# First image of a convolution and attention kernel: combined taps made earlier, 42 convolution products ahead of the maxima, and the queries' transfers asked for apart from those of the relative logits

## The chip, the cores and the metric

The kernel runs on one core of one Trainium2 chip, in float32. The metric is the device time of one execution in microseconds. Each version is run three times and its median is given. Beside that there is one execution taken by the hardware profiler, whose trace is what the profile shows.

## What is computed

The input is `x`, 8 images of 32 x 32 positions with 256 channels. Layer 0 works on each image by itself:

- a group normalization of the channels (groups of 8) over the whole image;
- a 3 x 3 convolution from 256 to 192 channels;
- beside it, attention over the 1024 positions with 8 heads of 8 channels. Its logits are `q.k` plus two relative terms, one that depends on the horizontal distance and the query, and one that depends on the vertical distance and the query;
- the two results are put side by side (192 + 64 channels) and added to `x`.

Layer 1 is a single-head attention over the 1024 positions of each image, and then a mixture of 8 experts of which 2 are taken for each image, with layer norms between. In the reference's words, the part that the change touches is

```python
logits = jnp.einsum('bnid,bnjd->bnij', qf, kf) + rel_w + rel_h
weights = jax.nn.softmax(logits, axis=-1)
conv_out = lax.conv_general_dilated(x, conv_w, (1, 1), 'SAME', ...) + conv_b
```

## The kernel before

**Stages.** The kernel takes the images one after the other. Of an image, the stages are: normalization (`norm_steps`), queries, keys, values and relative logits (`input_steps`), the attention of layer 0 with the convolution woven in (`conv_layer_attention`), and the attention of layer 1 (`attention_layer`). While one image is in its attention, the normalization and the input steps of the next one are run in pieces between the steps of the current one (`ahead`, `more`, `fill`). After the eighth image comes the expert stage.

**The convolution** is done along rows in groups of four outputs with the transform of a fast convolution: `conv_weights` makes six combined sets of taps (`convw`) from the three taps of a row, once in the program, and `by_fours` makes six combined inputs (`gdif`) for each image. `conv_weights` is six instructions of VectorE of 1152 elements (L277 to L290) with ScalarE's scalings between them. The convolution of an image is then 72 products (L515, `conv_steps`). A product is one matmul instruction in the program and two matmuls in the trace, since it is float32; the same holds for every matmul here. Every 12 products fill one PSUM tile `pc`, which ScalarE copies out (L524), and GpSimd adds the result to the image `T`.

**The attention of layer 0** is cut into four units (two groups of four heads, two halves of the queries). Each unit has a tile `F` of 128 partitions, which holds the moving operand of its logits in blocks of 32 rows for each head: 16 rows of the vertical relative logits (`F<-rh`), 8 rows of the queries (`F<-kq`), 8 rows of the horizontal relative logits, which later also take the maxima (`F<-rwd`, `F<-mb`). These rows are put there by DMA from the tiles `rh` and `kq` and from the DRAM tile `rwd`. In all that is 8 + 8 + 8 transfers for a unit, issued by SyncE (SP). The stationary operand is `km`: keys, copied in by 16 transfers `km<-kq` (L431), beside patterns of zeros and ones that GpSimd makes once, at the start, in 32 small instructions (`key_patterns`, L260 and L261).

**The steps of a unit.** A unit has 8 steps of *scoring*: two times two products `lg<-km,F` (L583), each pair followed by a maximum on VectorE (L591, 128x1024 elements). Then its maxima are turned and put into `F` (`fold`, L607 to L613), and 8 steps of *weighing* follow: products `st<-F,km` (L623), exponentials on ScalarE (L631) and products with the values (L640). Weighing lags by 10 steps (`lead = NT + LAG`), so in the first 10 steps of an image nothing is weighed, and what is left of the convolution is spread over them. Before the first step, `first` products of the convolution are issued:

```python
            first = min(left, 3 * KC)
            conv.run(first)
```

For the first image all 72 products are left, so 6 stand in front, and then 7, 7, 7, 7, 7, 7, 6, 6, 6, 6 follow the scores of the ten steps. For every other image 36 of 72 are left at that point, the rest having run in the attention of layer 1 of the image before: 6 in front and 3 after the scores of each step.

**The prologue.** The first image has no image before it in whose attention its normalization and input steps could run. Its order on TensorE and VectorE is the order of the calls: normalization, the first 12 pieces of `input_steps` (`pk` L396, `kq` L406 on ScalarE and L413 on VectorE, `pvv` L417, `vall` L436), then the tables of the relative logits (`reld_steps`, L236, eight instructions on VectorE), then one piece of `input_steps` after the other with three pieces of `other` behind each. `other` is `by_fours` and after it `conv_weights`. The pieces of `input_steps` in this part are the relative logits: products `prel` (L468) in four lots, each copied out of PSUM by VectorE and ScalarE together (L480, L482: two lots to `rw`, two to `rh`), then the transposes `tpw` (L493) and their copies to `rwq` (L495 VectorE, L497 ScalarE).

**What orders the rest.** TensorE keeps the order of the calls all through the eight images, VectorE in the prologue alone. Every other queue is ordered by the framework's scheduler, SP's and GpSimd's too. A queue runs in order: an instruction that waits holds those behind it. An SP transfer also waits until the transfer eight places before it has landed, since eight semaphores are used in turn.

**The buffers of F.** The tag `F` has three buffers, and the taps, the normalized image `x`, the relative logits `rw`, the units' `F` and two tiles of layer 1 take them in turn. In the first image the taps, `x` and `rw` have the three, and the first unit's `F` gets that of `x`: its transfers wait for the last instruction of `by_fours`.

Of the kernel before, what the change touches and what calls it, by code (L numbers as in the profile page):

```python
# [20 lines left out]
NT = S // P  # L21
KC = C // P
NH, DH, DK = 8, 8, 64
HG = 4
# [12 lines left out]
def kernel(  # L37
# [26 lines left out]
    nc = tc.nc  # L64
# [27 lines left out]
    with ExitStack() as ph:  # L92
# [32 lines left out]
        for n, table in (("h", key_rel_h), ("w", key_rel_w)):  # L125
# [19 lines left out]
        taps = work.tile([P, 4096], FP, tag="F", name="taps", bufs=3)[:, 0 : 9 * KC * CO]  # L145
        nc.scalar.dma_start(
            out=taps.rearrange("p (n o) -> p n o", o=CO), in_=conv_w.rearrange("a b (k p) o -> p (a b k) o", p=P)
# [121 lines left out]
        def conv_weights(taps):  # L269


            taps = taps.rearrange("p (a b n) -> p b a n", a=3, b=3)
            w0, w1, w2 = (taps[:, i] for i in range(3))
            cw = [convw[:, v] for v in range(NV)]
            nc.scalar.mul(cw[4], w0, 0.25)
            nc.scalar.copy(cw[5], w2)
            nc.vector.tensor_tensor(cw[1], w0, w2, ALU.add)  # L277
            yield
            nc.vector.tensor_tensor(cw[0], cw[1], w1, ALU.add)
            nc.scalar.mul(cw[0], cw[0], -1.0 / 6)  # L280
            yield
            nc.vector.tensor_tensor(cw[1], cw[1], w1, ALU.subtract)
            nc.scalar.mul(cw[1], cw[1], -1.0 / 6)
            yield
            nc.vector.scalar_tensor_tensor(cw[3], w2, 4.0, w0, ALU.mult, ALU.add)
            yield
            nc.vector.scalar_tensor_tensor(cw[2], w1, 2.0, cw[3], ALU.mult, ALU.add)
            nc.scalar.mul(cw[2], cw[2], 1.0 / 24)
            yield
            nc.vector.scalar_tensor_tensor(cw[3], w1, -2.0, cw[3], ALU.mult, ALU.add)  # L290
            nc.scalar.mul(cw[3], cw[3], 1.0 / 24)
            yield
# [92 lines left out]
        def input_steps(b, held):  # L385
# [3 lines left out]
            xn = held["xn"].rearrange("p k a c j x -> p k (a c j x)")  # L389
            kq = work.tile([P, S], FP, tag="kq", name="kq")  # L390
# [35 lines left out]
            for g in range(NG):  # L426
                for a in range(2):
                    for hl in range(HG):
                        r = 32 * ((hl + 2 * a) % HG) + 16
                        h = g * HG + hl  # L430
                        nc.sync.dma_start(  # L431
                            out=KM[g][r : r + DH, a].rearrange("p e k -> p (e k)"),
# [18 lines left out]
            rw = [rw[:, g * S : (g + 1) * S] for g in range(NG)]  # L451
            rwd = [drw.tile([P, S], FP, tag="rwd", name="rwd", bufs=2 * NG) for _ in range(NG)]
            rwq = work.tile([P, NT, NG, P], FP, tag="rwq", name="rwq")
            held.update(kq=kq, rh=rh, rwd=rwd, rwq=rwq)
            for which in range(2):
                for half in range(2):
                    prs = lg_tile("prel")
# [30 lines left out]
            for t2 in range(NT // 2):  # L488
# [7 lines left out]
                else:  # L496
                    nc.scalar.copy(rwq[:, t2 * 2 : t2 * 2 + 2], tp)  # L497
                yield 0.43, 0
            held["units"] = [Unit(0, kq, rh, rwd)]

        def conv_steps(b, place):

# [38 lines left out]
        class Unit:  # L541


            def __init__(self, n, kq, rh, rwd):
                self.g, self.half = divmod(n, 2)
                g, cols = self.g, slice(self.half * 512, self.half * 512 + 512)
                self.rh = rh[g][:, cols]


                self.F = f_tile("F")  # L550
                for a in range(2):
                    for hl in range(HG):
                        r = 32 * ((hl + 2 * a) % HG)
                        h = g * HG + hl
                        nc.sync.dma_start(
                            out=self.F[r : r + 16, a],
                            in_=rh[g][a * 64 + hl : a * 64 + 64 : HG, cols].unsqueeze(1).to_broadcast([16, 4, 512]),
                        )
                        nc.sync.dma_start(
                            out=self.F[r + 16 : r + 24, a],  # L560
                            in_=kq[DK + h * DH : DK + (h + 1) * DH, cols].unsqueeze(1).to_broadcast([DH, 4, 512]),
                        )
                for a in range(2):
                    for hl in range(HG):
                        r = 32 * ((hl + 2 * a) % HG)
                        nc.sync.dma_start(
                            out=self.F[r + 24 : r + 32, a],
                            in_=rwd[g].rearrange("(e j h) s -> h j e s", e=4, h=HG)[hl, :, :, cols],
                        )
                self.mx = work.tile([P, 4, HG], FP, tag="mx", name="mx", bufs=2)  # L570
                self.pts = {}
                self.po = None
# [108 lines left out]
        def conv_layer_attention(b, units, kq, rh, rwd, rwq, conv, early, ahead, more):  # L681

            at = work.tile([P, NT, DK], FP, tag="at", name="at")
            units.append(Unit(1, kq, rh, rwd))
            left = conv.left
            lead = NT + LAG  # L690
            first = min(left, 3 * KC)
            conv.run(first)
            left -= first
            for s in range(NU * NT + lead + 2):
                u, j = divmod(s, NT)
                w, k = divmod(s - lead, NT)
                g, l = divmod(s - lead - 1, NT)
                score, weigh, gather = u < NU, 0 <= w < NU, 0 <= g < NU


                if score:
                    units[u].score(2 * j, rwq)
                    if weigh:
                        units[w].weigh(k, (1,), st_tile)
                        units[w].weigh(k, (3,), st_tile)
                    if gather and l:
                        units[g].gather(l, (0, 1))
                    units[u].score(2 * j + 1, rwq)
                    if weigh:
                        units[w].weigh(k, (0,), st_tile)  # L710
                        units[w].weigh(k, (2,), st_tile)
                    if gather:
                        units[g].gather(l, (2, 3) if l else (0, 1, 2, 3))
                else:
                    if weigh:
                        units[w].weigh(k, (0,), st_tile)
                        units[w].weigh(k, (2,), st_tile)
                        units[w].weigh(k, (1, 3), lg_tile)
                    if gather:
                        units[g].gather(l, (0, 1, 2, 3))  # L720
                if g == NU:
                    more(KC, 0)
                if 0 <= g and g <= NU and l == 0 and g > 0:
                    units[g - 1].settle(at)
                if g == NU:
                    more(NT // 2, 0)
                if not weigh:
                    todo = -(-left // (lead - s))
                    conv.run(todo)
                    left -= todo  # L730
                if s == 5:
                    early()
                if s > NU * NT:
                    next(ahead, None)
                if s % NT == 0 and 0 < u <= NU:
                    units[u - 1].fold(u - 1)
                if s % NT == 0 and 0 < u < NU - 1:
                    units.append(Unit(u + 1, kq, rh, rwd))

            aT = pt_tile("aT")[0:DK, 0:S]  # L740
            for q in range(2):
                tp = st_tile("tpa").rearrange("p (j t) -> p j t", j=4)
                for j in range(4):
                    nc.tensor.transpose(tp[0:DK, j, :], at[:, q * 4 + j, :], ident)
                dst, src = aT[:, q * 512 : (q + 1) * 512], tp[0:DK].rearrange("p j t -> p (j t)")
                if q == 0:
                    nc.vector.tensor_copy(dst, src)
                else:
                    nc.scalar.copy(dst, src)
            more(KC, 0)  # L750
            pp = st_tile("pp").rearrange("p (t c) -> p t c", c=DK)
            for t in range(NT):
                nc.tensor.matmul(pp[:, t, :], lhsT=aT[:, t * P : (t + 1) * P], rhs=aw, start=True, stop=True)
            nc.vector.tensor_tensor(T[b][:, :, CO:C], pp, T[b][:, :, CO:C], ALU.add)
            more(0, 4)
# [199 lines left out]
        with tc.manual_schedule(engines={mybir.EngineType.PE, mybir.EngineType.DVE}):  # L955
            held = {}
            half_w, half_h, reld_steps = tables()
            for _ in norm_steps(0, held):
                pass
            KM = key_patterns()  # L960
            steps = input_steps(0, held)
            for _ in range(4 + NT):
                next(steps)
            reld_steps()
            other = chain(by_fours(held["xn"]), conv_weights(taps))
            for _ in steps:
                for _ in range(3):
                    next(other, None)
            for _ in other:
                pass  # L970
        with tc.manual_schedule(engines={mybir.EngineType.PE}):
            conv = Conv(0)
            means = []
            for b in range(B):
# [12 lines left out]
                now, held = held, {}  # L987
# [319 lines left out]
```

## Time and profile before

| what | value |
|---|---|
| median of 3 runs | 2448.43 us |
| the runs | 2446.56, 2448.43, 2452.04 us |
| the profiled execution | 2444.67 us, with a span of 2442.9 us |
| mean clock granted to TensorE | 0.981 |
| TensorE matmul (PE) | 2314.1 us busy, 95% of the span |
| VectorE (DVE) | 1485.5 us, 61% |
| ScalarE (ACT) | 1026.1 us, 42% |
| GpSimd (POOL) | 475.6 us, 19% |

The profile page gives busy time for each engine (matmuls are pipelined, so a busy PE isn't PE at its peak), a row of 40 slices of the span for each engine with the clock that TensorE was granted, and the costliest groups of instructions. The trace behind it answers with timelines (start, duration, engine, line, operation, and in brackets how long the engine had been idle and what released it), with tables of busy time by stretch, and with the shortest, median and longest duration of the instructions of one line.

### The profile page before, as it was taken

The numbers are of one execution on the slowest core, as the hardware profiler recorded it, in microseconds if no ns is written. First come the engines' busy times: TensorE is split into PE (matmuls) and PEld (weight loads), VectorE is DVE, ScalarE is ACT, GpSimd is POOL, SyncE is SP. The second block draws the span as 40 slices with busy tenths as digits, with TensorE's granted clock in tenths as the row PEclk, the third lists the DMA queues.
The fourth block names the chain that finished last, engine by engine and source line by source line (L and its number), as shares of the span: only waits on it lengthen the run. The fifth ranks groups of instructions, "written<-read, shape, count | busy, mean of one in ns | idle before, by whom it ended". The sixth has DMA issues, their size and how long they took to land. (4 is left out here: it accounts for less than half of the span.)

```text
span 2442.9 us, 41840 instructions
## 1 busy us (share of the span) xinstructions
PE 2314.1 (95%) x17273; PEld 1299.7 (53%) x17273; DVE 1485.5 (61%) x2661; ACT 1026.1 (42%) x1717; POOL 475.6 (19%) x446
## 2 busy tenths in 40 slices
PE   5999999999999999999999999999998879999998
PEld 4535643564366436643663376337632546666665
DVE  7776487548755875587467746774774434444443
ACT  2255336433643464346335732563266323222232
POOL 3202130213031202210230023002301032222221
PEclk7999999999999999999999999999999989999999
DMA  4521242134222412240324032403240032121210
GB/s 124 82 40 27 41 97 39 35 46 90 32 43 57 80 22 51 57 85 9 58 70 72 4 57 70 72 4 57 60 66 2 23 121 69 69 69 69 70 60 26
DMA packets 71468, 135.82 MB, mean 56 GB/s; under 512 B 12000, under 2 KB 24168, under 8 KB 69232
## 3 DMA queue, kind: packets, MB, share of 16 engines
q1 hardware_dynamic: 65488, 115.47, 23.7%
q0 software_dynamic: 3056, 15.73, 1.9%
q8 instruction: 136, 2.23, 0.4%
q10 hardware_dynamic: 2736, 1.97, 0.3%
q14 instruction: 52, 0.43, 0.1%
HBM read 53.43 MB, written 25.17 MB: 32 GB/s over the span
## 5 line engine op out<-in xcount | busy, mean ns | idle before, releaser
L591 DVE TENSOR_REDUCE my<-lg 128x32 f32<-128x1024 f32 x512 | 618.5, 1223 | 161.8 <-PE st L623 125.9
L631 ACT ACTIVATE PT<-st 128x512 f32<-128x512 f32 (+1 forms) x944 | 541.6, 633 | 306.2 <-PE st L623 301.7
L623 PE MATMUL st<-F,km 32*128 32x512 f32 x2048 | 545.2, 641 | 17.2 <-DMA F<-mb 11.9
L583 PE MATMUL lg<-km,F 24*128 24x512 f32 x2048 | 534.9, 637 | 6.1 <-DMA F<-kq 3.7
L640 PE MATMUL po<-PT,vall 128*32 128x256 f32 (+1 forms) x3200 | 315.1, 453 | 2.9 <-ACT PT L631 2.4
L583 PEld LDWEIGHTS lg<-km,F 24*128 24x128 f32 x2048 | 156.0, 183 | 186.5 <-issue 112.1
L515 PE MATMUL pc<-convw,gdif 128*128 128x192 f32 x1152 | 236.1, 345 | 11.5 <-ACT m L524 8.7
L640 PEld LDWEIGHTS po<-PT,vall 128*32 128x32 f32 x3200 | 66.9, 108 | 314.6 <-issue 280.1
L515 PEld LDWEIGHTS pc<-convw,gdif 128*128 128x128 f32 x1152 | 186.8, 192 | 81.5 <-issue 59.9
L623 PEld LDWEIGHTS st<-F,km 32*128 32x128 f32 x2048 | 177.5, 184 | 96.3 <-issue 43.5
L1220 PE MATMUL phd<-n2T,w 128*128 128x512 f32 x512 | 223.7, 594 | 0.0
L1237 PE MATMUL py<-w,hT 128*128 128x256 f32 x1024 | 223.6, 379 | 0.0
L1237 PEld LDWEIGHTS py<-w,hT 128*128 128x128 f32 x1024 | 194.6, 190 | 33.3 <-issue 7.4
L311 POOL TENSOR_TENSOR T<-T,l0b 128x2048 f32<-128x2048 f32 x8 | 36.4, 4546 | 633.5 <-PE tpx L304 633.5
L1220 PEld LDWEIGHTS phd<-n2T,w 128*128 128x128 f32 x512 | 97.0, 191 | 114.9 <-issue 107.7
L1244 DVE TENSOR_TENSOR r<-py,n 128x256 f32<-128x256 f32 x64 | 27.1, 423 | 215.0 <-PE py L1237 215.0
L863 PE MATMUL po<-pt,qkv 128*128 128x256 f32 x512 | 116.6, 381 | 11.3 <-DVE pt L855 11.3
L524 ACT COPY m<-pc 128x384 f32<-128x384 f32 x48 | 23.0, 479 | 247.3 <-PE pc L515 247.3
L1227 ACT ACTIVATE hT<-phd,b1c 128x512 f32<-128x512 f32 x128 | 86.3, 686 | 96.5 <-PE phd L1220 96.3
L841 DVE TENSOR_REDUCE nm<-lg 128x1 f32<-128x1024 f32 x64 | 78.1, 1220 | 77.5 <-PE lg L832 77.5
L780 POOL TENSOR_TENSOR T<-T,n 128x256 f32<-128x256 f32 x64 | 47.1, 743 | 372.8 <-DVE n L775 372.8
L832 PE MATMUL lg<-qkv 128*128 128x512 f32 x256 | 119.1, 593 | 0.0
(250 smaller groups left out, 2627.6 us busy)
## 6 DMA issues: line engine op xcount, KB each, us to landing
F<-rh SPq DMA_DIRECT2D x256, 128.0 KB
F<-kq SPq DMA_DIRECT2D x256, 64.0 KB
F<-rwd SPq DMA_DIRECT2D x256, 64.0 KB
w<-in_L_ffn_W_dram SPq DMA_DIRECT2D x32, 512.0 KB
rwd<-rw SPq DMA_DIRECT2D x16, 512.0 KB
Td<-T POOLq DMA_DIRECT2D x8, 1024.0 KB, 8.3
T<-Td SPq DMA_DIRECT2D x8, 1024.0 KB
out_dram<-yo SPq DMA_DIRECT2D x16, 512.0 KB
```

The costliest lines, as they stand in the source:

```text
L515: nc.tensor.matmul(pc[:, v, :], lhsT=gflat[:, 2 * pair + v, kc, at : at + P], rhs=convw[:, 2 * pair + v, dy, kc * CO : (kc + 1) * CO], sta ...
L583: nc.tensor.matmul(lg[:, a, :], lhsT=self.F[r : r + 24, a, 0, i * P : (i + 1) * P], rhs=KM[self.g][r : r + 24, a].rearrange("p e k -> p (e ...
L591: nc.vector.tensor_reduce(my[:, :, hl], lg.rearrange("p a (y x) -> p y a x", y=WW), AX.XY, ALU.max)
L623: nc.tensor.matmul(st[:, i, :] if len(heads) > 1 else st, lhsT=KM[self.g][r : r + 32, a, e, :], rhs=self.F[r : r + 32, a, e, :], start=Tru ...
L631: nc.scalar.activation(self.pts[j][:, hs, :], st, AF.Exp)
L640: nc.tensor.matmul(self.po[32 * hl : 32 * hl + 32, cols], lhsT=vall[:, j, h * (DH + 1) : h * (DH + 1) + 32], rhs=self.pts[j][:, hl, cols], ...
L832: nc.tensor.matmul(lg[:, h, :], lhsT=qk[0][:, i * P : (i + 1) * P], rhs=qk[1][:, h * 512 : (h + 1) * 512], start=True, stop=True,)
L841: nc.vector.tensor_reduce(nm, lg, AX.X, ALU.max, negate=True)
L863: nc.tensor.matmul(po[:, 0:IB], lhsT=v1[:, jc, :], rhs=pt[:, jc, :], start=jc == 0, stop=jc == NT - 1)
L1220: nc.tensor.matmul(phd, lhsT=ws[k][0][:, kc, f * P : (f + 1) * P], rhs=n2T[:, kc, q * 512 : (q + 1) * 512], start=kc == 0, stop=kc == KC - 1,)
L1227: nc.scalar.activation(hT[:, k * NF + f, :], phd, AF.Gelu, bias=b1c[:, f, k * B + b : k * B + b + 1])
L1237: nc.tensor.matmul(py, lhsT=hT[:, k * NF + f, j * P : (j + 1) * P], rhs=ws[k][1][:, f, :], start=k == 0 and f == 0, stop=k == TOPK - 1 and ...
```

## The change

There are three edits.

1. **Transfers of a unit in two parts.** `Unit` asks for the 8 transfers `F<-kq` when it is made. A new method `relate` asks for the 8 `F<-rh` and the 8 `F<-rwd`. For the first unit of an image the unit is now made as soon as `kq` is there, ahead of the relative logits, and `relate` is called at the end of `input_steps`. For the other units the two calls follow each other. Before, `F<-rh` and `F<-kq` alternated.
2. **`first = max(0, left - 3 * lead)`** in place of `min(left, 3 * KC)`. For the first image that is 72 - 30 = 42 products in front, and 3 after the scores of each of the ten steps. For the other images it is 36 - 30 = 6, as it was.
3. **The prologue's order.** `other` is now `conv_weights` and after it `by_fours`, and it is begun with the first piece of `input_steps`.

```diff
-            held.update(kq=kq, rh=rh, rwd=rwd, rwq=rwq)
+            held.update(kq=kq, rh=rh, rwd=rwd, rwq=rwq, units=[Unit(0, kq)])
...
-            held["units"] = [Unit(0, kq, rh, rwd)]
+            held["units"][0].relate(rh, rwd)
...
-            def __init__(self, n, kq, rh, rwd):
+            def __init__(self, n, kq):
                 self.g, self.half = divmod(n, 2)
-                g, cols = self.g, slice(self.half * 512, self.half * 512 + 512)
+                self.cols = slice(self.half * 512, self.half * 512 + 512)
+                self.F = f_tile("F")
+                for a, hl, r in self.places():
+                    h = self.g * HG + hl
+                    nc.sync.dma_start(
+                        out=self.F[r + 16 : r + 24, a],
+                        in_=kq[DK + h * DH : DK + (h + 1) * DH, self.cols].unsqueeze(1).to_broadcast([DH, 4, 512]),
+                    )
+            def places(self):
+                return [(a, hl, 32 * ((hl + 2 * a) % HG)) for a in range(2) for hl in range(HG)]
+            def relate(self, rh, rwd):
+                g, cols = self.g, self.cols
                 self.rh = rh[g][:, cols]
...
+                for a, hl, r in self.places():
+                    nc.sync.dma_start(
+                        out=self.F[r : r + 16, a],
+                        in_=rh[g][a * 64 + hl : a * 64 + 64 : HG, cols].unsqueeze(1).to_broadcast([16, 4, 512]),
+                    )
+                for a, hl, r in self.places():
+                    nc.sync.dma_start(
+                        out=self.F[r + 24 : r + 32, a],
+                        in_=rwd[g].rearrange("(e j h) s -> h j e s", e=4, h=HG)[hl, :, :, cols],
+                    )
...
-            units.append(Unit(1, kq, rh, rwd))
+            units.append(Unit(1, kq))
+            units[1].relate(rh, rwd)
...
-            first = min(left, 3 * KC)
+            first = max(0, left - 3 * lead)
...
-                    units.append(Unit(u + 1, kq, rh, rwd))
+                    units.append(Unit(u + 1, kq))
+                    units[u + 1].relate(rh, rwd)
...
-            for _ in range(4 + NT):
-                next(steps)
-            reld_steps()
-            other = chain(by_fours(held["xn"]), conv_weights(taps))
-            for _ in steps:
-                for _ in range(3):
+            other = chain(conv_weights(taps), by_fours(held["xn"]))
+            for n, _ in enumerate(steps):
+                if n + 1 == 4 + NT:
+                    reld_steps()
+                for _ in range((n < 4) + (n > 8) + (n >= 4 + NT)):
                     next(other, None)
```

In the built program this becomes the following. TensorE's order differs in the first image alone: 42 products in front and 3 after each step's scores. VectorE's differs in the prologue alone: the first of the six combinations of taps stands before the first half of `kq`, the next three between the two halves, the last two after the second half and before `vall`; `by_fours` has two pieces behind each piece of the relative logits where it had three, so fewer of its instructions stand between one copy of relative logits and the next. ScalarE's scalings of taps move with them; GpSimd's order is the same. On SP, for each image, one `F<-kq` of the first unit stands before the 16 `km<-kq`, the other seven behind them and before the two `rwd<-rw`, then come 8 `F<-rh` and 8 `F<-rwd`; every other unit has 8 `F<-kq`, 8 `F<-rh`, 8 `F<-rwd`. In the first image the first unit's `F` gets the buffer that nothing has used yet, `rw` that of the taps, and the second unit's `F` that of `x`. In the later images `rw` and the tiles of layer 1 follow each other as they did.

More of the change, by code (lines that the diff above doesn't have):

```diff
@@ L541 @@
         class Unit:
-            def __init__(self, n, kq, rh, rwd):
+            def __init__(self, n, kq):
                 self.g, self.half = divmod(n, 2)
-                g, cols = self.g, slice(self.half * 512, self.half * 512 + 512)
-                self.rh = rh[g][:, cols]
[L550 to L569, printed above, removed]
```

## The prediction

> **What bounds the kernel now.** I read the page's row of slices first. TensorE is busy at nine tenths or more in nearly every slice, at full clock; the first slice, 61 us long, is the exception, and the change rearranges just that part.
>
> ```profile
> span 2442.9 us, 41840 instructions
> PE   5999999999999999999999999999998879999998
> PEclk7999999999999999999999999999999989999999
> ```
>
> The table of stretches of 5 us (TensorE busy, weight loads, VectorE, ScalarE, GpSimd, TensorE's clock, DMA share, GB/s) says where in the slice time is lost: between 50 and 65 us TensorE does 2 to 3.4 us of 5, and from 60 to 70 it has half its clock.
>
> ```profile
> 50.00:55.00 5.00, 2.24 (x9) 2.01 (x7) 4.93 (x5) 3.22 (x4) 0.00 (x0) 0.80 0.54 118
> 55.00:60.00 5.00, 2.93 (x9) 1.87 (x8) 3.92 (x5) 2.33 (x2) 0.00 (x0) 0.84 0.69 114
> 65.00:70.00 5.00, 5.00 (x15) 4.34 (x14) 1.23 (x1) 0.46 (x1) 0.00 (x0) 0.50 0.58 81
> 70.00:75.00 5.00, 5.00 (x32) 3.19 (x32) 3.24 (x5) 0.01 (x1) 3.09 (x4) 0.99 0.59 88
> ```
>
> The timeline names what stands there (start, duration, instruction, idle time before it and what ended that).
>
> ```profile
> 47.06 3.17 PE L493 MATMUL tpw<-ident,rw 128*128 128x128 f32 x16
> 52.99 3.88 PE L515 MATMUL pc<-convw,gdif 128*128 128x192 f32 x12 [2.76 <-ACT convw L280]
> 61.58 3.78 PE L583 MATMUL lg<-km,F 24*128 24x512 f32 x6 [3.65 <-DMA F<-kq]
> 65.29 4.85 PE L515 MATMUL pc<-convw,gdif 128*128 128x192 f32 x14
> 71.14 2.54 PE L515 MATMUL pc<-convw,gdif 128*128 128x192 f32 x14
> 101.73 1.13 PE L583 MATMUL lg<-km,F 24*128 24x512 f32 x4
> 102.59 1.15 PE L623 MATMUL st<-F,km 32*128 32x512 f32 x6
> ```
>
> TensorE waits for the taps until 52.99, does 6 products, waits for transfers until 61.58, and does 7 products at half clock in 4.85 us that later take 2.54. From 71 on, nine steps of 3.5 us follow, bound by TensorE (2.54 of products, 1.0 of scores). The first weighing, at 102.59, is my mark: all 72 products are done there in both kernels, and what follows has the same order on every engine but SP. The gain or loss is what this mark moves.
>
> What the first steps cost with 3 products each can be read in the second image:
>
> ```profile
> 308.56 1.14 PE L583 MATMUL lg<-km,F 24*128 24x512 f32 x8
> 338.62 1.13 PE L583 MATMUL lg<-km,F 24*128 24x512 f32 x4
> 340.14 1.15 PE L623 MATMUL st<-F,km 32*128 32x512 f32 x6 [0.40 <-DMA F<-mb]
> ```
>
> Ten steps from 308.56 to 338.62 are 30.1 us, bound by VectorE (27.5 of 30 busy). They hold 0.7 of a token mean that the first image hasn't (L929, L932): 29.4. To the first weighing it is 1.5 more.
>
> **From the first product to the mark.** 42 products are 84 matmuls. In a run at full clock one follows the other after 0.162 us (2.54 for 14 holds the start and the tail), at half clock after 0.32. So 84 x 0.162 = 13.6. The transposes in front of them (L493, 3.2 us) brought full clock within 50 to 55 in this trace; I allow 0.9 for cold clock at the start (5 or 6 matmuls at 0.16 more), with 0 and 4.2 as ends (4.2 is half of the 8.5 us from 61.58 to 70.07, after which the clock rose). Then 29.4 and 1.5: 45.4 us from the first product to the first weighing. Before, it was 102.59 - 52.99 = 49.6. So 4.2 are won, if the first product still starts at 52.99. The 42 products also cover the transfers: eight `F<-rh`, asked for at 0.65 us each, are issued in 5.2 us, and the first product of scores comes 14.5 us after the first product.
>
> **When the first product starts.** It stands behind `tpw` and needs ScalarE's copy of the third of them, which stands behind the last copy of `rh`, and so depends on VectorE, which is now given the taps early. Six combinations of 1.36 us (L277 to L290) are 8.2 us; the taps are there from 15.9, where ScalarE's L275 reads them, and its four scalings of 1.16 lie in ScalarE's idle time before `rw`. The combinations are put where VectorE was idle for 2.56 and 3.37 us:
>
> ```profile
> 25.31 0.74 DVE L413 TENSOR_SCALAR kq<-pk,kqb 64x512 f32<-64x512 f32 x1 [2.56 <-ACT kq L406]
> 29.42 0.74 DVE L413 TENSOR_SCALAR kq<-pk,kqb 64x512 f32<-64x512 f32 x1 [3.37 <-ACT kq L406]
> ```
>
> If nothing else counted: first combination 22.7 to 24.0, `kq` at 25.3 as before, three combinations to 30.0, `kq` to 30.7, two to 33.3, `vall` to 34.0, the tables L236 at their distance of 0.27 to 36.1, two lots of `by_fours` of 2.1, and the first copy of `rw` at 38.2 instead of 36.45. But GpSimd makes the key patterns from 22.75 to 32.31, 32 instructions without a pause, and the duration lists (shortest, median, longest in ns) show what they do to VectorE:
>
> ```profile
> L236 DVE TENSOR_TENSOR reld<-bdh x8: 346/348/1510, 31.0 to 34.1; 128x192 f32<-128x192 f32 x8
> L261 POOL TENSOR_TENSOR km<-km,oh x16: 390/390/397, 23.2 to 31.9; 128x128 f32<-128x128 f32 x16
> L1250 DVE SCALAR_TENSOR_TENSOR yo<-r,fmv,T x4: 1130/2571/2575, 2036.0 to 2042.0; 128x256 f32<-128x256 f32 x4
> ```
>
> The first L236 took 1510 ns where 348 do, from 31.0 until just after GpSimd's last pattern. L1250, in the expert stage, takes 2571 (476 where GpSimd rests), each waiting for one GpSimd instruction of 2.5 us. So the two don't work at once here, and 9.6 us of GpSimd and 8.2 of VectorE must follow each other from 22.7 on. If they alternate, as for L1250, `kq` and `vall`, which read PSUM, lie beside GpSimd, half the patterns are made by `vall`'s end at 35.3, the tables and `by_fours` have one pattern of 0.3 before each: 8 x 0.57, then 4 x 0.58 and 2 x 0.8, first copy of `rw` at 43.7. If VectorE waits for all of the patterns, as L236 did: patterns to 33.5, five combinations, `kq`, `vall`, tables, `by_fours`: 45.6. I take alternation: L236's row is of the very same patterns but one case, L1250's holds in every image of that stage.
>
> *The Trainium skill, "SBUF — State Buffer", section "Who interferes with whom", says that a VectorE instruction with two SBUF inputs and a GpSimd instruction that reads SBUF exclude each other for a whole instruction. All six combinations have two, so the rule speaks against this change; by it the sum is that of 43.7 or 45.6, without it that of 38.2.*
>
> From the first copy of `rw` it is, by the timeline's distances: 3.6 to the second copy (before 4.7; four instructions of `by_fours` fewer stand between), 2.9 to the first `rh`, 3.4 to the second, then its 0.7, ScalarE's 0.6 for the other half and its wait for `tpw`, 0.6 copy, in all 2.6: 12.5. First product at 50.7, 56.2 or 58.1. Mark at 96.1, 101.6 or 103.5. Against 102.59: -6.5, -1.0 or +0.9.
>
> **Edits with no price.** SP's queue: `F<-kq` waits for ScalarE's `kq` (25.27), and `km<-kq` behind it for GpSimd's patterns, the last four until 44 if the two engines alternate. Behind them stand four transfers of 0.67, seven `F<-kq` of 0.7, two `rwd` and eight `F<-rh` of 0.65: issued by 59, 11 us before the first scores; without that cover each us counts whole. `rw` takes the buffer of the taps, which the sixth combination, earlier in VectorE's order, has left. The second unit's `F` waits for `by_fours`; its 24 transfers (20 us) are issued by 86 and used at 94, 23.5 us after the first scores. In later images the first unit's queries are asked for at 229 and used at 308; a later unit's transfers are issued in 18.4 us (130.2 to 148.6 for the fourth) and its scores start at 157: the order within the 18.4 has 8 us of cover. 0 for all, with 0.3 per image either way.
>
> **Forecast.** The profiled execution took 2444.67, 3.8 below the median (2448.43). Minus 1.0: 2443.7 on its scale, 2447.4 as a median. Its own range, from -3 (GpSimd always waits: first product at 50.7, but patterns, and behind them `F<-rh`, so late that the first scores stand until some 69) to +2 (VectorE always waits, a cold start): 2445 to 2450.5. Chance 0.54. 0.2%, about what a measurement of this kernel can tell from no change, is 4.9 us, so this case is "same".
>
> **Rivals.**
> - *The taps fill idle time.* GpSimd's patterns give way at no cost, first product at 50.7: -6.5, 2441.9. For it: 5.9 us of idle VectorE; against it: 1510 ns. Chance 0.30.
> - *The products run cold* (slower). TensorE has little to do between its second lot of `prel` (36.5) and `rw`'s copies; in this trace small matmuls from 32 to 45 left the clock at 0.5. At half clock a matmul costs 0.16 more. The forecast turns into slower by over 4.9 when 37 more of the 84 run cold; all of them: +13.6 - 0.9, 2460.1. 8.5 us cold, as at 61.58: 2450.7. Chance 0.10, of which 0.08 is slower.
> - *Transfers in the later images are late*, since every unit's are reordered. It decides once they land over 8 us later than now; from there each us is 21 over three units in each of seven images: 2468 with one. Against it: the cover above. Chance 0.06.
> - *It doesn't do what it says* holds in part: the products move in the first image alone, so nothing is repeated eight times.
>
> **Numbers.** 2447.4; range 2440.5 to 2453.5, from the first rival with a run's scatter of 1.4 to the second with some clock lost and VectorE waiting longest. Faster 0.33 (0.30, and 0.03 of the forecast's tail), same 0.53, slower 0.14.
>
> **What would show it.** Right: L277 to L290 longer than 1.36 each, or GpSimd's L260 and L261 stretched beyond 32.31; the first copy L480 near 44; products from 56 at 0.162 apart; first `lg` near 71 with no wait for `F`; first `st` near 101.6. Wrong: combinations of 1.36 with L480 at 38 (first rival); 84 matmuls in over 20 us (second); waits for DMA before `lg` in later images (third).

## The result, and what the profile after shows

Over 14 runs each, the changed kernel took 2448.16 us (median; 2443.08 to 2455.36), the kernel before 2451.2 us (2443.67 to 2452.15). The ratio is 0.9998, with a 95% interval of 0.9988 to 1.0008: no difference that can be measured. (The two medians alone would give 0.9988, but the runs of one kernel lie up to 8 us apart, those of the other up to 12.) The profiled execution took 2443.08 us, 1.6 less than that of before (2444.67).

The row of slices of the changed kernel, as it stands on the page:

```profile
span 2441.3 us, 41749 instructions
PE   6999999999999999999999999999998879999998
PEclk7999999999999999999999999999998989999999
```

Only TensorE's first digit has moved, from 5 to 6, and one digit of its clock late in the span has fallen. The stretches of the first slice (TensorE busy, weight loads, VectorE, ScalarE, GpSimd, TensorE's clock, DMA share, GB/s) show where:

```profile
50.00:55.00 5.00, 5.00 (x34) 4.71 (x31) 4.93 (x15) 1.66 (x3) 0.00 (x0) 0.56 0.83 181
55.00:60.00 5.00, 5.00 (x32) 5.00 (x32) 0.14 (x1) 0.48 (x1) 1.14 (x2) 1.00 0.99 196
65.00:70.00 5.00, 5.00 (x33) 3.94 (x31) 0.89 (x1) 0.48 (x1) 2.34 (x3) 1.00 0.53 68
70.00:75.00 5.00, 4.83 (x24) 2.10 (x22) 4.57 (x7) 0.48 (x1) 0.53 (x1) 1.00 0.54 69
```

TensorE hardly stands (4.83 us of 5 is the least), and from 55 it has its full clock, in place of 2 to 3 us of work in 5 and half the clock at 65. The timeline of TensorE in the same place:

```profile
50.23 3.67 PE L493 MATMUL tpw<-ident,rw 128*128 128x128 f32 x16
53.73 14.25 PE L515 MATMUL pc<-convw,gdif 128*128 128x192 f32 x84
67.91 1.14 PE L587 MATMUL lg<-km,F 24*128 24x512 f32 x8
97.05 1.13 PE L587 MATMUL lg<-km,F 24*128 24x512 f32 x4
99.31 1.15 PE L627 MATMUL st<-F,km 32*128 32x512 f32 x6 [1.14 <-DMA F<-mb]
```

The mark, the first weighing, is at 99.31 in place of 102.59: 3.3 us are won there. At the end of the span 1.6 are left. Between the two both kernels do the same work, so two questions are open: what made the 3.3, and where do they go?

Two groups of the page answer to the rival of late transfers in later images. The scores' idle time is 3.3 us in the whole kernel (6.1 before), and the largest part of it no longer comes from a DMA; the weighing stage waits 1.4 us more (17.2 before), of which 1.14 is the wait at the mark itself. Before, and then after:

```profile
L583 PE MATMUL lg<-km,F 24*128 24x512 f32 x2048 | 534.9, 637 | 6.1 <-DMA F<-kq 3.7
L623 PE MATMUL st<-F,km 32*128 32x512 f32 x2048 | 545.2, 641 | 17.2 <-DMA F<-mb 11.9
L587 PE MATMUL lg<-km,F 24*128 24x512 f32 x2048 | 535.4, 636 | 3.3 <-DVE my L595 1.3
L627 PE MATMUL st<-F,km 32*128 32x512 f32 x2048 | 546.3, 643 | 18.6 <-DMA F<-mb 13.3
```

### The profile page after: what moved, and what is told of

It reads as the page before. It is cut to its first block, busy times and chain, and to the rows that moved or that the text cites. A ratio compares the mean times of both kernels' runs of the same rounds, so it can differ in the third digit from the quotient of the medians.

```text
span 2441.3 us, 41749 instructions
## 1 busy us (share of the span) xinstructions
PE 2311.8 (95%) x17273; PEld 1294.8 (53%) x17273; DVE 1486.8 (61%) x2661; ACT 1026.2 (42%) x1717; POOL 486.3 (20%) x446
## 5 line engine op out<-in xcount | busy, mean ns | idle before, releaser
L1232 ACT ACTIVATE hT<-phd,b1c 128x512 f32<-128x512 f32 x128 | 86.3, 686 | 96.3 <-PE phd L1225 96.1
```

Source lines behind the costliest of these rows:

```text
L1232: nc.scalar.activation(hT[:, k * NF + f, :], phd, AF.Gelu, bias=b1c[:, f, k * B + b : k * B + b + 1])
```

## The experiments

*Theory A:* the 3.3 us are the products' own: 84 matmuls lie without a pause where TensorE waited for transfers and ran at half clock. *Rival B:* the other two edits made them, since taps and transfers come earlier, and the number of products in front doesn't matter. A second pair of theories concerns VectorE and GpSimd, a third the time behind the mark. All readings are of the mark unless the text says otherwise.

**How far a mark can be trusted.** Both kernels were run once more.

> The kernel before, unchanged, a second time, to learn how far one profile's mark can be trusted. If the prologue is the same from run to run: first product 53.0 and mark 102.6 within 0.3. If the clock's stretches fall differently (the projections L396 took 5.7 us in some of the runs here and 7.0 in others): up to 1.7 later at the mark. At the end of the images half-clock stretches in other places than at 442 and 681.

> The changed kernel, unchanged, a second time. Same prologue: mark 99.3 within 0.3, a gain of 3.3 over the kernel before in the same state of its projections; with the projections L396 at 7.0 us: about 100.7 to 101. The whole run's difference to the repeat of the kernel before is then the mark's plus 1.6 us for each half-clock stretch at an image's end that one has and the other has not.

Before: 102.89 (102.59 the first time). After: 99.30 (99.31). The projections L396 (the prologue's first large matmuls, which make keys and queries) took 5.5 to 5.7 us in all four. In three other runs below they took 7.0, at half clock, and the first product was later by about as much; this is told where it counts.

**Only the products** (the kernel before with 42 products in front):

```
-            first = min(left, 3 * KC)
+            first = max(0, left - 3 * lead)
```

> The kernel before with one line changed: all 42 products stand in front of the first image's scores, transfers and prologue order as before. Measure: the mark, the first weighing product (102.59 us before, 99.31 after). Theory A (the gain is made by the 84 matmuls lying without a pause between the transposes and the scores, where TensorE of the kernel before waited for transfers and ran its first products and scores cold): first product at 53.0 as before, scores at about 67.5, mark 98.5 to 99.5, all of the gain. Rival B (the gain is made by F's transfers and the taps being earlier, the number of products in front does not matter): mark 102 to 103.

100.91: between the theories. Its timeline and two of its stretches of 3 us (columns as above):

```profile
53.21 16.87 PE L515 MATMUL pc<-convw,gdif 128*128 128x192 f32 x84 [2.25 <-ACT convw L280]
100.91 1.15 PE L623 MATMUL st<-F,km 32*128 32x512 f32 x6 [0.50 <-DMA F<-mb]
```

```profile
53.00:56.00 3.00, 2.79 (x9) 2.79 (x10) 2.96 (x4) 1.79 (x3) 0.00 (x0) 0.50 0.65 122
56.00:59.00 3.00, 3.00 (x11) 3.00 (x10) 2.97 (x4) 2.13 (x2) 0.00 (x0) 0.50 0.68 117
```

The 84 matmuls took 16.8 us to the first score, not 14.2. They started earlier than in the changed kernel, but behind a pause of 2.25 us for the combined taps, and the clock stayed at 0.50 until 59 (x11 in 3 us, where the changed kernel has x20 at 1.00 from 56 to 59). So the products won 1.7 in this run, not 3.3.

How much of the lost 2.6 us belongs to the pause, one run can't tell. The clock changes only at steps of 3.4 us (last section), and where the steps lie differs from run to run. The kernel before has the same prologue and a pause of 2.76 us in front of its first products; there the clock was full during the pause, at half from 53 and full again from 56.4, 2.8 us sooner than here:

```profile
50.00:53.00 3.00, 0.24 (x4) 0.01 (x1) 2.93 (x3) 1.58 (x2) 0.00 (x0) 1.00 0.47 113
53.00:56.00 3.00, 3.00 (x9) 3.00 (x10) 2.97 (x4) 1.64 (x2) 0.00 (x0) 0.50 0.64 116
56.00:59.00 3.00, 1.93 (x6) 0.87 (x5) 2.95 (x4) 2.33 (x2) 0.00 (x0) 0.93 0.70 117
```

With the steps of that run the 42 products would have ended some 1.4 us sooner (half of 2.8), and the mark would be near 99.5, where theory A had it: an estimate from these rows, not a run.

**Only the other two edits** (the changed kernel with 6 products in front):

```
-            first = max(0, left - 3 * lead)
+            first = min(left, 3 * KC)
```

> The changed kernel with 6 products (12 matmuls) in front of the scores again and 7 in each of the next steps; transfers in two parts and the new order of the prologue stay. Theory A: TensorE has 12 matmuls (2 us) from 53.7, then waits for F's late scores, whose transfers land near 58 to 61; the wait and cold matmuls take back what was gained: mark 101.5 to 103. Rival B: the two edits that stay make the gain: mark at 99.3 or before it. If the ten steps simply follow from 58 to 61 at the 3.53 us a step that 7 products a step took later in the trace of before, the mark is at 94 to 97, and then the 42 products in front cost time.

TensorE's timeline:

```profile
55.21 2.22 PE L515 MATMUL pc<-convw,gdif 128*128 128x192 f32 x12 [0.24 <-ACT rwq L497]
59.44 1.09 PE L587 MATMUL lg<-km,F 24*128 24x512 f32 x2 [2.02 <-DMA F<-rh]
64.06 3.03 PE L587 MATMUL lg<-km,F 24*128 24x512 f32 x6 [3.53 <-DMA F<-rh]
67.02 4.69 PE L515 MATMUL pc<-convw,gdif 128*128 128x192 f32 x14
104.13 1.15 PE L627 MATMUL st<-F,km 32*128 32x512 f32 x6
```

104.13, of which some 1.4 are the projections at 7.0 us: about 102.7, the time of before. With few products in front `F` is late by 2.0 and 3.5 us, and behind the wait 7 products (14 matmuls) take 4.69 us, at half clock. Rival B falls: taps and transfers that come earlier win nothing alone.

**Products and the new order of the prologue, transfers as before** (the run with only the products, and in it the third edit):

```
-            other = chain(by_fours(held["xn"]), conv_weights(taps))
+            other = chain(conv_weights(taps), by_fours(held["xn"]))
...
```

> The changed kernel with its first edit undone everywhere: a unit's transfers of queries and of relative logits are asked for together again, interleaved, after the logits; the 42 products in front and the new order of the prologue stay. So this is the 42-products run (first products at 53.2 after TensorE stood 2.25 us for the combined taps, mark 100.91) plus the taps first. If the split of the transfers is worth nothing while 42 products cover the wait for F: 84 products in a row with the transposes in front of them, in 14.2 to 14.5 us, and the mark at 99.3 to 99.8 (or 1.35 later if TensorE's projections L396 start cold, 7.0 us in place of 5.7, as they did in two of the runs). If the split is what lets the scores start: SyncE ends the 16 interleaved requests near 64.5, they land 5 to 6 us later, scores wait until 70 and the mark is 101 to 102.

TensorE's timeline:

```profile
53.94 13.92 PE L515 MATMUL pc<-convw,gdif 128*128 128x192 f32 x84 [0.24 <-ACT rwq L497]
98.73 1.15 PE L623 MATMUL st<-F,km 32*128 32x512 f32 x6 [0.54 <-DMA F<-mb]
```

98.73: 0.6 *earlier* than the changed kernel. Put together, by edits (products 2, prologue 3, transfers 1):

| edits | first product | mark |
|---|---|---|
| none (two runs) | 52.99, 53.13 | 102.59, 102.89 |
| 2 | 53.21 | 100.91 |
| 2 and 3 | 53.94 | 98.73 |
| 1, 2 and 3 (two runs) | 53.73, 54.11 | 99.31, 99.30 |
| 1 and 3 | 55.21 (projections at half clock) | 104.13 |

So, in these runs, the products alone win 1.7 and the new order of the prologue, beside them, 2.2 more: it puts the products right behind the transposes, and the clock rises at 53 to 54 in place of 59. The sum of 3.9 is firmer than its parts: one run stands behind each, and by the estimate above they would be 3.1 and 0.8. That the clock comes later behind a pause holds in all three runs that have one (both of the kernel before and the one with only the products: 56.4, 56.9 and 59.3, against 53.1 to 54.4 in the three without).

The split of the transfers costs 0.6 at the mark. All of that 0.6 is the wait for `F<-mb` (1.14 and 1.08 us, against 0.54), although both kernels ask for it at 95.4. The second unit's last transfers are asked for until 92.4 with the split and until 88.3 without, and from 93 to 95, just before `F<-mb` is asked for, the DMA engines are still 0.55 busy with the split and 0.01 without (the last number but one):

```profile
93.00:95.00 2.00, 2.00 (x15) 1.36 (x15) 2.00 (x3) 0.00 (x0) 0.00 (x0) 1.00 0.55 57
93.00:95.00 2.00, 2.00 (x15) 1.40 (x15) 2.00 (x3) 0.00 (x0) 0.00 (x0) 1.00 0.01 2
```

Two runs below (the patterns early, with 42 products) keep the split and ask for all of this earlier. Their DMA is idle from 93 to 95 (0.00 in both), and the wait for `F<-mb` is 0.56 and 0.55 us. So it is the late transfers that cost the 0.6, not the split by itself.

**Fewer products in front:**

```
-            first = max(0, left - 3 * lead)
+            first = 24 if b == 0 else max(0, left - 3 * lead)
```

> The changed kernel with 24 products (48 matmuls, 48 x 0.17 = 8.2 us) in front in place of 42; the other 18 go among the next steps. 24 end at about 62, which is just after F's late scores land (58 to 61), so that nothing waits, and the steps that follow hold matmuls in gaps that the 42-product version leaves to VectorE's maxima. If TensorE waits in those steps for VectorE or for slots anyway (gap theory): mark 94 to 97. If the matmuls of a step merely add to the step (sum theory): mark 99.3 as with 42. If SyncE's queue decides (the transfer behind the second image's F ends near 95.4): mark 96.3 at the earliest.

99.45, with the projections at 7.0 us and the first product at 55.08. From the first product it is 44.4 us, 1.2 less than with 42, though the scores now wait for `F`, as the timeline has it:

```profile
64.78 1.96 PE L587 MATMUL lg<-km,F 24*128 24x512 f32 x6 [0.58 <-DMA F<-rh]
```

It lies between the gap theory and the sum theory: from the first scores' end to the last scores in front of the mark it is 31.4 us (66.67 to 98.06) in place of 28.1, with 36 matmuls more, 5.8 us at 0.162. So 2.5 of the 5.8 us fit into gaps that TensorE has in these steps anyway, and 3.3 lengthen them.

**GpSimd's patterns out of VectorE's way** (this run leaves out the first image's bias addition on GpSimd):

```
+            KM = key_patterns()
             for _ in norm_steps(0, held):
                 pass
-            KM = key_patterns()
...
+                if i:
+                    nc.scalar.copy(km.rearrange("p a e k -> p (a e k)"), KM[0].rearrange("p a e k -> p (a e k)"))
```

> The changed kernel with GpSimd's patterns (the one-hots into km) moved in front of the normalization and km's second buffer copied by ScalarE; the addition of the relative-position bias on GpSimd in the first image is left out. So GpSimd does nothing beside VectorE's combinations, tables and by-fours. Contention theory: VectorE's eight L236 copies come back from a pitch of 0.36 to 0.48 us to 0.27, the first copy of rw starts at 38.1 in place of 40.19, the first product at 51.6 in place of 53.73, mark 97.2. Rival (the VectorE delay has another cause): rw's copy stays at 40.2 and the mark at 99.3.

In the changed kernel VectorE and GpSimd had met like this, by the timeline (GpSimd's instructions one by one) and, for one line, by the list of durations (shortest, median and longest in ns):

```profile
25.69 1.34 DVE L279 TENSOR_TENSOR convw<-convw,taps 128x1152 f32<-128x1152 f32 x1
25.29 1.90 POOL L260 COPY km<-oh 128x128 f32<-128x128 f32 x1
27.07 1.36 DVE L282 TENSOR_TENSOR convw<-convw,taps 128x1152 f32<-128x1152 f32 x1
27.16 1.53 POOL L261 TENSOR_TENSOR km<-km,oh 128x128 f32<-128x128 f32 x1
28.34 1.56 DVE L285 SCALAR_TENSOR_TENSOR convw<-taps 128x1152 f32<-128x1152 f32 x1
28.65 1.52 POOL L261 TENSOR_TENSOR km<-km,oh 128x128 f32<-128x128 f32 x1
40.19 1.02 DVE L480 COPY rw<-prel 128x512 f32<-128x512 f32 x1
```

```profile
L236 DVE TENSOR_TENSOR reld<-bdh x8: 437/496/575, 33.7 to 36.6; 128x192 f32<-128x192 f32 x8
```

With the patterns early, by the same two views:

```profile
39.04 1.02 DVE L485 COPY rw<-prel 128x512 f32<-128x512 f32 x1
52.13 14.65 PE L520 MATMUL pc<-convw,gdif 128*128 128x192 f32 x84
97.53 1.15 PE L632 MATMUL st<-F,km 32*128 32x512 f32 x6 [0.56 <-DMA F<-mb]
```

```profile
L236 DVE TENSOR_TENSOR reld<-bdh x8: 350/355/357, 34.8 to 36.6; 128x192 f32<-128x192 f32 x8
```

97.53, close to the contention theory's 97.2. From the first combination to the first copy of `rw` it is 15.58 us (23.46 to 39.04), against 17.54 in the changed kernel (22.65 to 40.19): GpSimd's patterns cost VectorE 2.0 us there. The copy itself came at 39.04, between the 38.1 of the one theory and the 40.2 of the other, mostly because the combinations began 0.8 us later here: a subtraction of the normalization (L324), beside GpSimd's differences of the tables, took 1.80 us in place of 0.18. And 0.6 of the 1.8 us at the mark is the shorter wait for `F<-mb`.

**The same, complete,** with the addition held back to the end of the prologue:

```
+            nc.vector.tensor_copy(l0b, l0b)      # behind the last copy of rwq
+            nc.gpsimd.tensor_tensor(T[0], T[0], l0b.to_broadcast([P, NT, C]), ALU.add)
```

> Patterns early as before (GpSimd has no work beside VectorE's combinations, tables and by-fours), but complete: the first image's bias addition on GpSimd (4.5 us) is done at the end of the prologue, held back by a copy of the bias on VectorE after the last rwq copy; 42 products in front. If the addition fits into GpSimd's idle stretch in front of the first inverse transform (52 to 57.6): mark 97.5 as without it. If it delays the first products' slots or VectorE: later than that by what it delays, up to 99.3.

98.90, in a run whose projections took 7.0 us; from the first product to the mark 45.3, as without the addition (45.4). The addition is hidden: it starts at 55.39, when the products are under way, so the late first product (53.64 against 52.13) isn't its doing.

**The same with 24 products in front:**

> As the early patterns with the bias addition late, with 24 products in front in place of 42. F's late scores land near 59 to 60 there, 48 matmuls from 52.1 end at 60.2. With 24 in front the ten steps took 0.25 us a step more and the front 6.1 us less, so the mark is 3 to 3.5 us sooner if nothing waits for F: 95 to 96.5, against 97.5 with 42 (the run with 24 gained only 1.2 us from its first product to the mark, with 0.6 us of wait for F and a cold stretch in it). Whole time: 6 to 7 us less than before at the mark, the rest of the kernel unchanged: ratio 0.997 (0.995 to 0.999 with the scatter of some 1.6 us per cold stretch later on).

TensorE's timeline:

```profile
52.33 8.32 PE L520 MATMUL pc<-convw,gdif 128*128 128x192 f32 x48
60.58 1.14 PE L592 MATMUL lg<-km,F 24*128 24x512 f32 x8
94.02 1.15 PE L632 MATMUL st<-F,km 32*128 32x512 f32 x6 [0.26 <-DMA F<-mb]
```

94.02: 8.6 us earlier than in the kernel before. `F` is there when it is wanted, since SP's `km<-kq` end at 40.0 in place of 45.7. Over 11 runs it took 2445.32 us against 2449.65 (21 runs), ratio 0.9984 (0.9970 to 0.9998): a gain of 0.16%, just outside what can be told from no change, with half of the 8.6 us left. It is called the best version below, for its early mark.

It was run once more:

> Early patterns, late bias addition, 24 products in front, a second time. Same prologue: mark 94.0 within 0.3; with the projections at 7.0 us: 95.4 to 95.7. Whole run 6 to 9 us under the repeat of the kernel before, plus or minus 1.6 for each half-clock stretch that only one has.

Mark 93.19, outside the expected 0.3: one program's mark can differ by 0.8 (0.7 of it is there at the first product, 51.62 against 52.33). The whole time was 2444.74, more than the first time's profile (2435.42); why is told below.

**All of the tables' differences on GpSimd:**

```
-                    eng = nc.vector if j % 2 else nc.gpsimd
+                    eng = nc.gpsimd
```

> As the one before, with the eight L236 differences of VectorE (2.2 us at 34.8) also on GpSimd, right behind its seven (3.9 us at 15.3), so until about 23.6, beside the normalization. If the two engines do not hold each other there: VectorE is free 2.2 us earlier for the by-fours, first product near 50, mark 93 to 94.5. If they hold each other as in the run of after (GpSimd's operations became 2 to 5 times as long, VectorE's chain of tables 2 us longer) VectorE's normalization or GpSimd's differences take the 2.2 us back: mark 95 to 97.

The timelines of GpSimd, VectorE and TensorE:

```profile
15.30 8.18 POOL L236 TENSOR_TENSOR reld<-bdh 128x192 f32<-128x192 f32 x15
17.37 6.13 DVE L324 TENSOR_TENSOR dm<-gmv,gm 128x2 f32<-128x2 f32 x1
98.21 1.15 PE L632 MATMUL st<-F,km 32*128 32x512 f32 x6 [0.26 <-DMA F<-mb]
```

98.21, worse than either expectation. VectorE's subtraction of 2 elements, with two inputs in SBUF, started at 17.37 and ended with GpSimd's last difference, 6.1 us later. Ratio 0.9995 (0.9985 to 1.0005).

**Where the gain goes behind the mark.** An image of the changed kernel, from projections to projections, takes 237.5 us or 239.1. In the long ones the granted clock is at half for one stretch of 3.4 us at the image's end. The best version's two runs show it in the table of stretches, 4 us at the ends of three images. The repeat:

```profile
434.00:438.00 4.00, 4.00 (x23) 0.89 (x24) 4.00 (x13) 2.15 (x4) 0.00 (x0) 0.57 0.00 0
673.00:677.00 4.00, 4.00 (x23) 0.93 (x24) 4.00 (x13) 2.20 (x4) 0.00 (x0) 0.57 0.02 4
912.00:916.00 4.00, 4.00 (x23) 0.96 (x24) 4.00 (x13) 2.20 (x5) 0.00 (x0) 0.57 0.00 0
```

And the first run:

```profile
434.00:438.00 4.00, 4.00 (x35) 1.01 (x32) 4.00 (x12) 3.57 (x7) 0.00 (x0) 1.00 0.00 0
673.00:677.00 4.00, 4.00 (x36) 1.01 (x32) 4.00 (x13) 3.59 (x6) 0.00 (x0) 1.00 0.00 0
912.00:916.00 4.00, 4.00 (x33) 0.98 (x29) 4.00 (x15) 3.74 (x6) 0.00 (x0) 1.00 0.00 0
```

One program, two runs: the repeat meets a stretch at six of its first seven image ends, the first run at none, and the repeat is 9.3 us longer although its mark is the earlier one. So I counted, for each profile, in the record of the granted clock, the 3.4 us of half clock between the mark and the end of the eighth image, and put 1.5 us on each, and one constant (2337.3, from before) behind the mark:

| run | mark | stretches | mark + 2337.3 + 1.5 each | span |
|---|---|---|---|---|
| before | 102.59 | 2 | (2442.9) | 2442.9 |
| before again | 102.89 | 7 | 2450.7 | 2450.2 |
| after | 99.31 | 3 | 2441.1 | 2441.3 |
| after again | 99.30 | 5 | 2444.1 | 2443.9 |
| products only | 100.91 | 3 | 2442.7 | 2442.4 |
| 6 in front | 104.13 | 9 | 2454.9 | 2454.6 |
| 24 in front | 99.45 | 1 | 2438.3 | 2438.2 |
| patterns early | 97.53 | 4 | 2440.8 | 2440.3 |
| transfers as before | 98.73 | 5 | 2443.5 | 2443.0 |
| patterns early, complete | 98.90 | 6 | 2445.2 | 2446.0 |
| best | 94.02 | 1 | 2432.8 | 2433.6 |
| best again | 93.19 | 7 | 2441.0 | 2442.9 |
| differences on GpSimd | 98.21 | 1 | 2437.0 | 2437.5 |

Twelve spans follow within 1.9 us, most within 0.6 (the repeat of the best version has one more such stretch in the expert stage, behind the eighth image). So whole times differ by the mark and by the number of these stretches, 1 to 9 of them, and that number alone is worth 12 us. The profiled runs of before and after had 2 and 3: of the 3.3 us one more stretch took about 1.5 back.

## Why the prediction was right, and where it was off

The forecast was 2447.4 us and "same", by a gain of 1.0 at the mark; the median is 2448.16 (0.8 more), the class holds. But the steps did not all hold, and the close number is partly luck. The forecast started from 2448.43, the median of three runs of the kernel before; over 14 runs it is 2451.2, from where a gain of 1.0 leads to 2450.2. The gain at the mark was three times as large, and the start 2.8 too low. The low end of the forecast's own range, -3, was reached too, but by another route than its own (first product at 50.7, scores that stand until 69): the first product came at 53.73, the scores without a wait at 67.91.

- **From the first product to the mark:** forecast 45.4, measured 45.58. The parts: 84 matmuls 14.2 (14.5 with the cold start), ten steps 29.14 (29.4), to the first weighing 2.26 (1.5). The last one was short by 0.7, the wait for `F<-mb`; the run without the split has 0.6 us less of it. That VectorE bounds the ten steps, as the forecast read it, is true in part: with 5.8 us of matmuls more they became 3.3 longer.
- **The first product:** forecast 56.2, measured 53.73. This is the term that was mis-sized. I had VectorE and GpSimd alternate, and so the first copy of `rw` at 43.7, 5.5 us behind the sum without contention. It came at 40.19, 2.0 behind. They did alternate: each pattern instruction that met a combination ended 0.1 to 0.3 us after it. What was wrong is the price of a turn. The combinations paid next to nothing (1.34 to 1.56 us each, and `vall` ended at 33.8, not 35.3); it was GpSimd that waited, with patterns until 43.0 in place of 32.3. In the tables, VectorE's instructions followed each other after 0.36 to 0.50 us, as against 0.57 in the sum and 0.27 without GpSimd: a turn cost 0.1 to 0.2 us, where I had put the whole pattern instruction, 0.3. The prediction's own list of signs had the stretched patterns ("or GpSimd's L260 and L261 stretched beyond 32.31"), but its sum took the other engine to pay. From the copy of `rw` to the first product it was 13.5, 1.0 more than forecast. Together: 2.5 earlier, and the mark 2.3 earlier than forecast. The first rival (no cost at all, mark at 96.1) was 3.2 off on the other side.
- **The rule of the Trainium skill** ("SBUF — State Buffer", section "Who interferes with whom") that the two engines exclude each other is borne out: the patterns moved away gave 2.0 us. It adds that the order of issue decides who is blocked, each time for a whole instruction. Beside the combinations that fits: GpSimd waited for one at a time, at most 1.90 us. With all of the differences on GpSimd it does not: VectorE stood for 6.13 us through eleven of them, 0.59 us each.
- **Edits at no price:** `F<-rh` was issued by 60.1 (forecast 59). The second unit's transfers were issued by 92.4, not 86, and no score waited for them; but, still under way at 95.4, they cost the 0.6 us at `F<-mb` that I had put at nothing.
- **Rival "products run cold":** didn't hold for the changed kernel, but was near. Without the new order of the prologue the same products lost 2.6 us to the clock in the one run of it. I had priced that order by the first product's start alone and missed that it removes a pause in front of the products.
- **Rival "late transfers later":** no; the scores' idle time fell.
- **What I left out:** the time behind the mark. I took it as equal in both kernels. Here one run's half-clock stretches can outweigh the whole edit. The interval of the ratio ends at 0.9988, or 2.9 us, so it does not even hold the full 3.3. Whether the changed kernel meets more of these stretches on average, or whether this is chance, stays open: runs that weren't profiled show only a mean clock.

## What to carry to other kernels

Work that is put in front of a wait is worth more if it follows without a pause on what TensorE did before: the same 84 matmuls won 3.9 us so, and 1.7 behind a pause of 2.25 (one run each, and the place of the clock's steps has a part in it); look for the pause before counting the work. Where two engines exclude each other, it is not enough to know that they take turns: read from a run what a turn costs each of them. Here VectorE's long combinations paid nearly nothing, GpSimd's short patterns up to 1.6 us each, and in another order one VectorE subtraction paid for a whole row. And where an edit is worth less than the kernel's own scatter, judge it at a mark inside the program, then say what the rest of the program adds.

## What the runs showed of the hardware

- VectorE and GpSimd, both reading SBUF, held each other up, and not always in the same way. In the changed kernel they took turns: beside VectorE's combinations (1.34 to 1.56 us) GpSimd's 128-element copies and additions were up to 1.9 us long (0.28 and 0.39 alone), each until just after one combination's end. With all of the differences on GpSimd, one VectorE subtraction of 2 elements waited for eleven of them, 6.13 us (0.16 to 0.18 in the two kernels). Why it got no turn there, these runs don't tell.
- TensorE's half-clock stretches come in steps of 3.4 us (3.4, 6.8, 10.2, 13.7, 17.1 in these records). An image with one takes 239.0 us, which is 70 such steps; an image without takes 237.5, which is not a whole number. And they come mostly in rows, at the ends of 2 to 6 images one after the other, 238.9 or 239.0 us apart (2 in the kernel before, 6 in the repeat of the best version): an image that is 70 steps long brings the next end to the same place among these steps. That reading comes from these numbers alone; it was not tried. The Trainium skill ("TensorE: Matmul & The Clock Gate", Part 1) tells of a free-running window of about 3.4 us and calls its effect run-variable; it puts the penalty below 1% of a kernel. That agrees: 12 us between the runs with most and fewest stretches are 0.5%, but it is more than the change was worth.
